# A macaron block on one core: routing in one tabled order, and float16 halves transposed by transfers

## The chip, the cores and the metric

The kernel runs on one core of a Trainium2 chip. The metric is the device time of one execution in microseconds; the figure for the kernel before is a median of three runs, 2352.42 us (2351.3 to 2353.59). Engines are named as the profile names them: PE (TensorE matmuls), PEld (its weight loads), DVE (VectorE), ACT (ScalarE), POOL (GpSimd) and SP (SyncE, which here only issues transfers).

## The reference

The input x is [2, 4096, 512] in float32. Three residual steps follow one another:

```python
x = x + 0.5 * ffn(layernorm(x))      # 1: routing, GRU, and alpha @ values
x = x + attn(layernorm(x))           # 2: gated delta rule over 4096 tokens
x = x + 0.5 * ffn(layernorm(x))      # 3: same weights as 1

def ffn(x):                          # 64 slots, hidden 256, top 8
    ctx = concat([x, mean(S)])                        # S: the 64 slots
    h = gelu(ctx @ w1.T + b1)
    logits = (h @ w2.T + b2) / (abs(tau) + 0.1)
    alpha = softmax over the 8 largest logits, 0 elsewhere
    slot_input = alpha.T @ x / alpha.sum(tokens)      # needs all tokens
    S_new = GRU(slot_input, S)
    return alpha @ (S_new @ wv.T + bv) @ wo.T + bo

def attn(x):                         # 16 heads of 32
    q, k = l2norm(x @ Wq), l2norm(x @ Wk); v = x @ Wv
    a, b = sigmoid(x @ Wa + ba), sigmoid(x @ Wb + bb)
    # per token: error = v - state k; state = a state + (b error) k; y = state q
    return (rmsnorm(y, g_norm) * silu(x @ Wg)) @ Wo
```

The slots' new values depend on every token of a batch, so each FFN is a pass that routes all tokens, a short GRU, and a second pass that adds `alpha @ values` to x. The second pass of step 1 is merged into the attention, that of step 3 is the end of the kernel.

## The kernel before, in words

The tokens go in 32 blocks (`NBLK`) of 128 tokens for each of the two batches (`NB`), so a block is a tile of 128 partitions by 2 x 512 float32, 512 KB. The stages follow each other: the routing of the first FFN (`ffn_a_phase(..., "a", ...)`), its GRU (`gru`), the attention (`attention`), the routing of the second FFN (the same function with "c"), its GRU, and the last pass (`after_c`).

**Products in halves.** Products that need float32 are made from float16 halves: a value is scaled and split into `hi`, its float16 rounding, and `lo`, the rounding of what is left. `mm3` issues three float16 matmuls for one product, L128 (hi x hi), L129 (hi x lo) and L130 (lo x hi), so these three lines carry all such products whatever stage they belong to. Weights are split once by `split16`: an ACT activation (L176) for the high half and a DVE operation (L177) for the low one.

**Routing.** It runs in ten groups of blocks (`split_blocks`: one block, seven groups of four, two, one). A group has six stages. `a_load` reads x. `a_stats` makes mean and variance on DVE. `a_norm` normalizes on DVE, casts the high half `xh` on ACT (L383) and subtracts the low half `xl` on POOL (L385). The hidden layer contracts over the 512 features, so it needs both halves feature-major, with features on partitions: for each block 16 PE transposes of 128 x 128 (L394) write to PSUM (`fpt`), and ACT (L397, high) and DVE (L399, low) copy them to `xTh` and `xTl`. `a_hidden` makes the hidden layer (`mm3`), its gelu on ACT (L417) and the logits. `a_topk` finds the top 8 and the softmax (DVE L431 to L458, an exponential on ACT, one addition on POOL). `a_slots` transposes alpha, keeps it (`alpha_out` stores it to HBM for the attention, `alpha_keep` keeps it in SBUF), and adds alpha.T @ x to sums in PSUM.

The order in which these stages of different groups are issued comes from fractions: each stage is a generator that yields how far it has come, each has a start and an end in units of a group (the dictionary `PA`), and `run_merged` keeps the generators on a heap and always advances the one that is earliest. Each engine executes its own instructions in the order of issue. The weights' setup (`setup_hidden`, `setup_gh`, `setup_attention`) is merged into the first routing in the same way (`extra_a`). All loads and stores of the routings are issued on SP's queue.

**Attention.** It is a software pipeline over the 32 blocks. `run_pipe` walks through a table (`PIPE`, 287 steps), where `qk0.5` means: advance the generator of stage `qk0` for the block five ahead of the current one by one step. Inside `tc.manual_schedule()` that is the order of issue. The stage `load` reads x and alpha. `prep` adds the first FFN's result to x (`ffn_b`: two matmuls, L488 and L489, and a DVE addition), stores x1, and makes the LayerNorm; then, for each batch, four float32 PE transposes (L814) fill a PSUM tile `apt`, ACT casts it to `xTh` (L816) and DVE subtracts to get `xTl` (L818). `qk0`, `qk1` and `vg` are the projections (L128 to L130). `post0`, `post1`, `bpart`, `decays`, `xk`, `dx`, `kk`, `dec`, `solve` and `chain` are the delta rule in chunks of 32 tokens. `tail` normalizes y by a square root on ACT, multiplies by Wo (L1080, tiles `apo`), adds the residual (DVE L1083) and stores x2. XK, Vt, Gt and x1 are read back from HBM on SP's queue, behind the stores that come before them in the order of issue. In PSUM three buffers of tag `pj` are shared by the projections, `ffn_b` and `apo`.

**Last pass.** `KEEP` blocks of x2 stay in SBUF from the second routing; the others are read again, `F3X` buffers of them, `F3L` blocks ahead.

Of the kernel before, what the change touches and what calls it, by code (L numbers as in the profile page):

```python
# [19 lines left out]
P = 128  # L20
D = 512
# [13 lines left out]
HEAD, TAIL = 1, 1  # L35
CFG = {"a": dict(XT=7, XN=2, XH=10), "c": dict(XT=4, XN=2, XH=11)}
KEEP = 12
F3A, F3X, F3L = 4, 11, 8
# [14 lines left out]
def split_blocks(n):  # L53

    cuts = [0] + list(range(HEAD, n - TAIL, GB)) + [n - TAIL, n]
    cuts = sorted(set(cuts))
    return [(a, b - a) for a, b in zip(cuts, cuts[1:])]


def run_merged(items):  # L60

    heap = [(s0, i, None) for i, (s0, s1, g) in enumerate(items)]
    heapq.heapify(heap)
    while heap:
        _, i, g = heapq.heappop(heap)
        s0, s1, f = items[i]
        if g is None:
            g = f()
        try:
            heapq.heappush(heap, (s0 + next(g) * (s1 - s0), i, g))  # L70
        except StopIteration:
            pass


def run_pipe(tc, stages, n):
# [3 lines left out]
    for w in PIPE.split():  # L79
        w, _, m = w.partition("*")  # L80
        name, lead = w.split(".")
        order += [(name, int(lead))] * int(m or 1)
    live = {}
    with tc.manual_schedule():
        for k in range(-max(lead for _, lead in order), n):
            for name, lead in order:
                t = k + lead
                if 0 <= t < n:
                    if (name, t) not in live:
                        live[name, t] = stages[name](t)  # L90
                    next(live[name, t], None)


@with_exitstack
def tile_macaron(
# [82 lines left out]

    isc1 = cp.tile([P, 1], F32, tag="isc1", name="isc1")
# [51 lines left out]
    def setup_gh(gp, big, ppj):  # L231
# [3 lines left out]
        whht = big.tile([P, KC, 3 * D], F32, tag="big", name="whht")  # L235
        for k in range(KC):
            nc.sync.dma_start(whht[:, k], whh[k * P:(k + 1) * P])
# [3 lines left out]
        nc.sync.dma_start(bsum, bhh.rearrange("(k p) -> p k", p=P))  # L241
        V.tensor_tensor(bsum[:, 0:8], bsum[:, 0:8], bihn[:, 0:8], ALU.add)
        ghb = gp.tile([P, 12, NS], F32, tag="ghb", name="ghbs")
        yield 0.1
        for g in range(12):
            pg = ppj.tile([P, NS], F32, tag="tr", name=f"pgh{g}")
            for k in range(KC):
                nc.tensor.matmul(pg, whht[:, k, g * P:(g + 1) * P], hsT[:, k], start=(k == 0), stop=(k == KC - 1))
            V.tensor_scalar(ghb[:, g], pg, bsum[:, g:g + 1], None, ALU.add)
            yield 0.1 + 0.9 * (g + 1) / 12  # L250
        nc.sync.dma_start(ghd, ghb)

    def setup_attention(gp, big, ppj):
# [5 lines left out]
        yield 0.1  # L259
        scales(gp, ppj, [s1[:, :, 0:2 * D], s1[:, :, 2 * D:]], scA[:, 0:2], iscA[:, 0:2], "wq")  # L260
        yield 0.3
        for k in range(KC):
            for s, i in ((slice(0, 2 * D), 0), (slice(2 * D, NQ), 1)):
                o = [W[n_][:, k, s] for n_ in ("wqh", "wql")]
# [903 lines left out]
```

## Time and profile before

| what | value |
| --- | --- |
| median of three runs | 2352.42 us |
| profiled execution, its own time | 2342.8 us |
| span of its instructions | 2341.0 us |
| mean granted TensorE clock | 0.960 |
| PE busy | 2100.5 us (90%) |
| PEld busy | 1585.4 us (68%) |
| DVE busy | 1911.3 us (82%) |
| ACT busy | 1148.9 us (49%) |
| POOL busy | 808.5 us (35%) |
| DMA traffic | 302.75 MB, mean 129 GB/s |
| first routing, its GRU | 0 to 275, to 301 us |
| attention | 301 to about 2003 us |
| second routing, its GRU | 2004 to 2252, to 2280 us |
| last pass | 2280 to 2341 us |

The profile is one execution. Its page gives busy time by engine, a strip of the span in 40 slices with a digit for the busy tenths of each (PEclk: the clock that was granted to PE), and groups of instructions by line: busy time, mean duration in ns, and then the idle time just before them on their engine with what ended it. Engines overlap, so shares don't add up to the span. A matmul's duration overlaps that of its neighbours.

### The profile page before, as it was taken

The page shows a single profiled execution, that of the slowest core. Times are in us where ns is not written, and L with a number is a line of the kernel's source. Part 1 is how long each engine was busy: PE and PEld are TensorE (multiplying, and loading weights), DVE is VectorE, ACT ScalarE, POOL GpSimd, SP SyncE. Part 2 cuts the span into 40 slices and gives each one's busy share as a digit, 9 for nine tenths or more (in the row PEclk, how much of TensorE's full clock was granted, in tenths as well). Part 3 has the DMA queues.
Part 4 walks back from the last instruction along what each step waited for, and adds up shares of the span by engine and source line. Part 5 has one row for each costly group of instructions (what it writes and reads, how often), then busy time and mean ns, then how long its engine had stood idle before and what let it go on. Part 6 is the DMA issues. An engine that isn't in the chain of part 4 may idle for free. (4 is left out here: it accounts for less than half of the span.)

```text
span 2341.0 us, 101047 instructions
## 1 busy us (share of the span) xinstructions
PE 2100.5 (90%) x44989; PEld 1585.4 (68%) x44989; DVE 1911.3 (82%) x4876; ACT 1148.9 (49%) x1957; POOL 808.5 (35%) x750
## 2 busy tenths in 40 slices
PE   5878878999999999999999999999999976588886
PEld 5767757767777676777767677777667754377774
DVE  7898538988888888888889888888888886489656
ACT  4677445544445444444545444554444421367631
POOL 2333114433334343333434333444333441134300
PEclk9898989999999999999999999999999988799997
DMA  6332323344443344343334444344444332630049
GB/s 212 123 127 91 96 87 129 119 133 130 142 134 126 123 136 132 128 150 121 126 124 139 128 136 148 120 127 132 135 128 146 102 97 70 219 110 29 2 149 368
DMA packets 176516, 302.75 MB, mean 129 GB/s; under 512 B 27984, under 2 KB 73552, under 8 KB 176080
## 3 DMA queue, kind: packets, MB, share of 16 engines
q1 hardware_dynamic: 161728, 256.45, 32.9%
q10 hardware_dynamic: 14352, 39.85, 5.2%
q8 instruction: 352, 5.77, 1.2%
q14 instruction: 84, 0.69, 0.1%
HBM read 189.23 MB, written 107.00 MB: 127 GB/s over the span
## 5 line engine op out<-in xcount | busy, mean ns | idle before, releaser
L1080 PE MATMUL apo<-wo,Gt 128*128 128x512 f32 x512 | 279.1, 630 | 24.5 <-DVE x1r L1083 24.5
L128 PE MATMUL pv<-xTh,wgh 128*128 128x256 f16 x1024 | 282.1, 275 | 0.0
L129 PE MATMUL pv<-xTh,wgl 128*128 128x256 f16 x1024 | 280.2, 274 | 0.1
L130 PE MATMUL pv<-xTl,wgh 128*128 128x256 f16 x1024 | 280.3, 274 | 0.0
L1014 POOL TENSOR_TENSOR ps<-ST,AC 128x256 f32<-128x256 f32 x128 | 105.5, 824 | 442.4 <-DVE ST L1038 442.4
L128 PE MATMUL pq<-wqh,xTh 128*128 128x384 f16 (+1 forms) x768 | 242.8, 316 | 1.5 <-issue 0.8
L129 PE MATMUL pq<-wqh,xTl 128*128 128x384 f16 (+1 forms) x768 | 240.9, 314 | 0.2 <-DVE xTl L818 0.2
L130 PE MATMUL pq<-wql,xTh 128*128 128x384 f16 (+1 forms) x768 | 240.7, 313 | 0.0
L862 POOL TENSOR_TENSOR qk<-qk,rn 128x512 f32<-128x512 f32 x128 | 137.6, 1075 | 231.7 <-issue 106.7
L836 ACT ACTIVATE qk<-pq,iscA 128x384 f32<-128x384 f32 (+1 forms) x192 | 105.4, 549 | 162.5 <-PE pq L130 139.5
L980 POOL TENSOR_TENSOR KQ<-KQ,Ax 128x512 f32<-128x512 f32 x128 | 168.4, 1315 | 0.4 <-PE pa L959 0.4
L764 DVE TENSOR_TENSOR tmp<-N,MT 128x256 f32<-128x256 f32 (+7 forms) x384 | 161.2, 426 | 5.6
L758 DVE TENSOR_TENSOR tmp<-N,U 128x256 f32<-128x256 f32 (+7 forms) x384 | 164.0, 434 | 1.4
L838 ACT ACTIVATE sq<-pq,iscA 128x384 f32<-128x384 f32 (+1 forms) x192 | 164.7, 858 | 0.0
L1018 PEld LDWEIGHTS pc<-KQ,S 32*32 32x32 f32 x8192 | 123.2, 106 | 50.6 <-ACT Y L1044 31.0
L760 DVE TENSOR_REDUCE MT<-tmp 128x32 f32<-128x256 f32 (+7 forms) x384 | 153.8, 407 | 0.0
L959 PE MATMUL pa<-KQ 32*32 32x64 f32 x8192 | 143.6, 217 | 11.2 <-ACT KQ L872 4.9
L1018 PE MATMUL pc<-KQ,S 32*32 32x64 f32 x8192 | 142.8, 217 | 9.5 <-DVE S L1040 4.9
L959 PEld LDWEIGHTS pa<-KQ 32*32 32x32 f32 x8192 | 121.7, 105 | 37.9 <-issue 14.9
L1035 PEld LDWEIGHTS pc<-X,u 32*32 32x32 f32 x8192 | 120.7, 105 | 38.6 <-issue 21.9
L1035 PE MATMUL pc<-X,u 32*32 32x64 f32 x8192 | 141.9, 216 | 5.2 <-ACT u L1032 3.7
L917 ACT ACTIVATE vg<-pv,iscA 128x512 f32<-128x512 f32 x128 | 88.1, 688 | 96.7 <-PE pv L130 88.7
(304 smaller groups left out, 5760.3 us busy)
## 6 DMA issues: line engine op xcount, KB each, us to landing
d<-a0d ACTq DMA_DIRECT2D x32, 528.0 KB
Ax<-a0d ACTq DMA_DIRECT2D x32, 528.0 KB
xt<-in_x_dram SPq DMA_DIRECT2D x32, 512.0 KB
x<-in_x_dram SPq DMA_DIRECT2D x64, 256.0 KB
x1d<-x SPq DMA_DIRECT2D x64, 256.0 KB
vtd<-vg SPq DMA_DIRECT2D x64, 256.0 KB
kd<-qk SPq DMA_DIRECT2D x64, 256.0 KB
XK<-kd SPq DMA_DIRECT2D x256, 64.0 KB
```

The costliest lines, as they stand in the source:

```text
L128: nc.tensor.matmul(po, lh, rh, start=start, stop=False, skip_group_check=True)
L129: nc.tensor.matmul(po, ll, rh, start=False, stop=False, skip_group_check=True)
L130: nc.tensor.matmul(po, lh, rl, start=False, stop=stop, skip_group_check=True)
L758: V.tensor_tensor(tv, vw(f, o10 + j0, [[C, n], [0, h], [1, ni]]), vw(U, ou + j0 * 17, [[0, n], [16, h], [1, ni]]), ALU.mult)
L760: yield lambda tv=tv, j0=j0: V.tensor_reduce(vw(mt, n * j0, [[1, n], [n, h]]), tv, AX.X, ALU.add)
L764: V.tensor_tensor(tv, vw(f, o11 + r0 * C, [[C, h], [0, n], [1, nk]]), vw(mt, 0, [[0, h], [n, n], [1, nk]]), ALU.mult)
L838: nc.scalar.activation(sq[:, f0:f1].rearrange("p (q g e) -> p q e g", g=NG, e=C), pq[:, 0:f1 - f0].rearrange("p (q e g) -> p q e g", g=NG, ...
L959: nc.tensor.matmul(pa[s, m], KQ[s, 0, c, b, g], KQ[s, :, c, b, g], start=(m == 0), stop=True, skip_group_check=True, tile_position=(32 * q ...
L980: nc.gpsimd.tensor_tensor(kc, kc, bass.AP(Ax.tensor, Ax[:, :, c].offset, [list(a[0]), [1, 2], list(a[1]), [1, C]]), ALU.mult)
L1018: nc.tensor.matmul(pcv[s, b, g, 0:2 * C], S[s, b, g], KQ[s, :, c, b, g], start=(g == 0), stop=False, skip_group_check=True, tile_position=tp)
L1035: nc.tensor.matmul(pcv[s, b, g, C:3 * C], u[s, b, g], d["X"][s, :, m], start=False, stop=True, skip_group_check=True, tile_position=tp)
L1080: nc.tensor.matmul(po, Gt[:, k, b], wo[:, k], start=(k == 0), stop=(k == KC - 1))
```

## The change

It has eight parts.

1. Both routings are issued by `run_pipe` with a table, `ROUTE`: 102 steps for a group (4 of load, 10 of stats, 24 of norm, 28 of hid, 20 of topk, 16 of slots), inside `tc.manual_schedule()`. `run_merged` and `PA` go. The setup of the weights is merged in between the steps (`extra`). The groups become one block, three, six of four, three, one: ten again.
2. In `a_norm` the 16 PE transposes of a block and their two copies out of PSUM go. Two `nc.sync.dma_start_transpose` per block, one of `xh` and one of `xl` (128 x 1024 float16, 256 KB each), write the feature-major tiles from SBUF to SBUF.
3. In the attention's `prep` the eight float32 PE transposes of a block go, with ACT's cast and DVE's subtraction from PSUM. ACT casts the token-major tile, POOL subtracts the low half, and four `dma_start_transpose` of 128 KB per block are issued on SP's queue.
4. The attention's weights are split by `split16p`: ACT scales in place, ACT copies the high half, POOL subtracts the low one. DVE has no part in it any more.
5. The routings' loads of x and of x2 and the stores of alpha are issued on ACT's queue.
6. PSUM in the attention: two buffers for the projections in place of three, and one of its own (`ppo`) for `ffn_b`, `pr` and `apo`. Most pools get `reuse_waits="tile"`, and a new pool `we` takes a part of the attention's tiles.
7. Sizes: `XT` 7 in both routings (4 in the second before), `XH` 9 (10 and 11 before), `KEEP` 11, `F3X` 14, `F3L` 11.
8. `PIPE` is a new table of 289 steps.

```diff
-HEAD, TAIL = 1, 1
-CFG = {"a": dict(XT=7, XN=2, XH=10), "c": dict(XT=4, XN=2, XH=11)}
-KEEP = 12
-F3A, F3X, F3L = 4, 11, 8
+HEAD, TAIL = (1, 4), (4, 1)
+CFG = dict(XT=7, XN=2, XH=9)
+KEEP = 11
+F3A, F3X, F3L = 4, 14, 11
...
+    def split16p(hi, lo, src, s):
+
+        nc.scalar.mul(src, src, s)
+        nc.scalar.copy(hi, src)
+        nc.gpsimd.tensor_tensor(lo, src, hi, ALU.subtract)
...
-                items += extra(gp, ptr, gw, NBLK / GB)
-                run_merged(items)
+                run_pipe(tc, stages, ng, ROUTE, extra(gp, ptr, gw, ng))
...
             nc.scalar.copy(xh, xn)
-            yield (j + 0.2) / blocks[1]
+            yield
+            nc.sync.dma_start_transpose(xTh, flat(xh))
+            yield
             nc.gpsimd.tensor_tensor(xl, xn, xh, ALU.subtract)
-            yield (j + 0.4) / blocks[1]
-            xTh = wp.tile([P, KC, NB * P], F16, tag="xTh", name=f"fxTh{u}", bufs=3)
-            xTl = wp.tile([P, KC, NB * P], F16, tag="xTl", name=f"fxTl{u}", bufs=3)
-            d["xT"].append((xTh, xTl))
-            for src16, dst, eng in ((xh, xTh, 0), (xl, xTl, 1)):
-                pt = ptr.tile([P, KC, NB * P], F16, tag="tr", name=f"fpt{u}_{eng}")
-                for k in range(KC):
-                    for b in range(NB):
-                        nc.tensor.transpose(pt[:, k, b * P:(b + 1) * P], src16[:, b, k * P:(k + 1) * P], ident16)
-                    yield (j + 0.4 + 0.3 * eng + 0.07 * (k + 1)) / blocks[1]
-                if eng == 0:
-                    nc.scalar.copy(dst, pt)
-                else:
-                    V.tensor_copy(dst, pt)
-                yield (j + 0.7 + 0.3 * eng) / blocks[1]
+            yield
+            nc.sync.dma_start_transpose(xTl, flat(xl))
+            yield
...
-        nc.sync.dma_start(xt, xr[t * P:(t + 1) * P])
+        nc.scalar.dma_start(xt, xr[t * P:(t + 1) * P])
...
-        nc.sync.dma_start(ald[t], aT.bitcast(F32))
+        nc.scalar.dma_start(ald[t], aT.bitcast(F32))
...
-            nc.sync.dma_start(xt, x2d[t * P:(t + 1) * P])
+            nc.scalar.dma_start(xt, x2d[t * P:(t + 1) * P])
...
+        ppo = pool("a1o", 1, space=PSUM)
         ptr = pool("a1t", 2, space=PSUM)
-        ppj = pool("a1p", 3, space=PSUM)
+        ppj = pool("a1p", 2, space=PSUM)
...
-                po = ffn_b(ppj, d["aT"], b, f"a{t}")
+                po = ffn_b(ppo, d["aT"], b, f"a{t}")
...
-                pt = ptr.tile([P, KC, P], F32, tag="tr", name=f"apt{t}_{b}")
-                for k in range(KC):
-                    nc.tensor.transpose(pt[:, k], xs[b][:, k * P:(k + 1) * P], ident)
-                yield
-                nc.scalar.copy(xTh[:, :, b], pt)
-                yield
-                V.tensor_tensor(xTl[:, :, b], pt, xTh[:, :, b], ALU.subtract)
+                xh = we.tile([P, D], F16, tag="xh", name=f"xh{t}_{b}", bufs=2)
+                nc.scalar.copy(xh, xs[b])
+                yield
+                nc.sync.dma_start_transpose(xTh[:, :, b], xh)
+                yield
+                xl = we.tile([P, D], F16, tag="xl", name=f"xl{t}_{b}", bufs=2)
+                nc.gpsimd.tensor_tensor(xl, xs[b], xh, ALU.subtract)
+                yield
+                nc.sync.dma_start_transpose(xTl[:, :, b], xl)
                 yield
...
-                po = ppj.tile([P, D], F32, tag="pj", name=f"apo{t}_{b}")
+                po = ppo.tile([P, D], F32, tag="pj", name=f"apo{t}_{b}")
```

## The prediction

> **What bounds the kernel now.** First the page's strips, for the stages.
>
> ```profile
> PE   5878878999999999999999999999999976588886
> DVE  7898538988888888888889888888888886489656
> PEclk9898989999999999999999999999999988799997
> DMA  6332323344443344343334444344444332630049
> ```
>
> Each digit is 58.5 us. Routing of the first FFN fills about the first five, the second's the five before the last two; in between is the attention, with PE at 9 throughout. The view by windows (columns: stretch, its length, busy PE, weight loads, DVE, ACT, POOL, granted clock, DMA share, GB/s) puts numbers on it:
>
> ```profile
> 0.00:275.00 275.00, 211.72 (x2491) 189.46 (x2491) 225.10 (x612) 172.85 (x245) 84.59 (x56) 0.92 0.37 123
> 25.00:275.00 250.00, 207.27 (x2472) 185.39 (x2472) 211.57 (x572) 168.44 (x239) 82.98 (x45) 0.91 0.33 108
> 477.00:1800.00 1323.00, 1294.62 (x32323) 937.53 (x32327) 1158.16 (x2918) 642.06 (x1171) 520.33 (x520) 1.00 0.41 132
> 2004.00:2252.00 248.00, 192.63 (x2370) 169.59 (x2370) 186.03 (x528) 158.78 (x220) 83.37 (x46) 0.89 0.23 82
> 2089.00:2199.00 110.00, 90.25 (x1175) 80.60 (x1176) 96.88 (x269) 82.50 (x112) 46.40 (x23) 0.97 0.06 21
> ```
>
> 477 to 1800 is the attention in its steady state: 26 blocks of 50.9 us, PE busy 98%, DVE 88%. So PE sets it. 2089 to 2199 is the second routing's steady state: 16 blocks (128 of its 256 L394 transposes) of 6.9 us, and there DVE leads with 88%, PE has 82%, ACT 75%. The first routing has DVE at 85% over 250 us. Third, the groups by shape, for what goes:
>
> ```profile
> L814 PE MATMUL apt<-ident,x 128*128 128x128 f32 x256 | 38.9, 275 | 10.0 <-ACT x L810 10.0
> L816 ACT CAST xTh<-apt 128x512 f16<-128x512 f32 x64 | 37.5, 586 | 57.4 <-PE pv L129 35.6 <-PE apt L814 21.7
> L818 DVE TENSOR_TENSOR xTl<-apt,xTh 128x512 f16<-128x512 f32 x64 | 43.7, 683 | 29.6 <-ACT xTh L816 21.5 <-PE pv L130 8.1
> L399 DVE COPY fxTla<-fpta 128x1024 f16<-128x1024 f16 x32 | 21.9, 686 | 15.5 <-PE fpta L394 15.4
> L397 ACT COPY fxTha<-fpta 128x1024 f16<-128x1024 f16 x32 | 32.3, 1010 | 4.9 <-PE fpta L394 4.7
> L385 POOL TENSOR_TENSOR xla<-fxna,xha 128x1024 f16<-128x1024 f32 x32 | 69.0, 2162 | 119.6 <-ACT xha L383 108.5 <-DVE s1a L448 11.1
> L177 DVE SCALAR_TENSOR_TENSOR wql<-wq,scA,wqh 128x256 f16<-128x256 f32 x16 | 13.8, 967 | 0.0
> L177 DVE SCALAR_TENSOR_TENSOR wgl<-wg,scA,wgh 128x512 f16<-128x512 f32 x8 | 6.7, 859 | 0.0
> ```
>
> A matmul's own 275 ns overlaps its neighbours. What a transpose takes of PE's stream is seen in the timeline, from its start to the next one's:
>
> ```profile
> 1002.12 0.60 PE L814 MATMUL apt<-ident,x 128*128 128x128 f32 x4
> 1002.55 0.29 PE L128 MATMUL pq<-wqh,xTh 128*128 128x288 f16 x1
> ```
>
> Four take 0.43 us; another set (1024.49 to 1025.02) 0.53.
>
> **The change part by part.** *Attention.* Eight transposes a block leave PE: 0.43 + 0.53 = 0.96 us, 31 us over 32 blocks. DVE loses 2 x 0.68 = 1.4 us a block, so it goes from 44.5 to 43.1 of 50 and doesn't take over. ACT casts from SBUF in place of PSUM: half of a 1.05 us L383 cast, 0.53 against 0.59, nothing. POOL gains two subtractions of half L385's size, 2.2 us on 20 of 50.9; it is hidden by its 30 idle us, and if it weren't the 2.2 would show in full. Four transfers of 128 KB join SP's queue, each behind its cast or subtraction; behind them wait the stores of qk, v and gate and the loads of XK, Vt, Gt and x1. SP idles in waits for most of its time now, so a late transposing input costs only where such a load is late already: DVE waits 44.7 us in all for x1r at L1083. By the new table the first half lands some 30 of 289 steps (5 us) before its first matmul, the second about 50 steps (9 us). PSUM goes from three shared buffers to two for the projections and one for the output matmuls; PE waits on L1083 for that buffer today (23.5 us in the steady state), and I expect that to change hands, not to go. I take the 31 us.
>
> *Second routing.* DVE loses L399 (0.68 of its 96.88 / 16 = 6.05 us a block), leaving 5.37. At the share of today, 88%, a block takes 6.10, 0.77 less: 25 us over 32. ACT's 5.16 loses 1.01 and gains a load's issue, 0.33: 4.5, hidden under DVE. PE loses 16 transposes of about 55 ns. At its start, the x2 loads stand on SP behind the last store of the attention; DVE waits 9.5 us for the first. In the changed order they stand on ACT, right behind the tail's last square root (1991 us now, 14 us earlier), so this wait can go; the transposing way to the first hidden layer is a little longer than 1.03 us of PE and 1.01 of ACT. I take 7.
>
> *First routing.* DVE's 225.1 loses 21.9 (L399) and 21.4 (L177: 13.8, 6.7 and 0.9 for small pieces): 182. ACT's 172.9 loses 32.3, gains the in-place scaling (same shapes as L176's 11.4, 5.4 and 1.2: 18.0) and 64 issues of 0.33 (21): 180. POOL gains 8,320 elements a partition at L385's 2.11 ns: 17.6 on 84.6, hidden. With two engines level, ACT's 168.4 - 32.3 + 18 + 21 = 175 at the 85% that DVE has today fills 206 of the 250 us: -44. ACT never reaches that share now (67%), so I take 40.
>
> *The rest.* One x2 block more is read again (KEEP 11): 0.5 MB at the last window's 353 GB/s, +1.5. The 102 pieces and the finer release of buffers have no row of their own: between -25 (a routing whose DVE stalls fall from 12 to 5%, both FFNs) and +25 (they grow as much); taken at 0.
>
> *The price of a transposing transfer* is in no row. The page's row of the hardware queue has packets, MB and the share of 16 engines' time:
>
> ```profile
> q1 hardware_dynamic: 161728, 256.45, 32.9%
> ```
>
> Below: 256.45 MB in 32.9% of 2341 us is 333 GB/s, so 256 KB take 0.8 us. Above: that queue's mean packet takes 76 ns (0.329 x 2341 x 16 / 161,728); one such for each of 1,024 source rows of 128 halves, over 16 engines, is 4.9 us. Same bytes, same engines, both ends on chip: nearest to the first; I take 1.6. A routing block has two, 3.2 us of DMA in 6.1, hidden. [...]
>
> **Sum.** -31 - 25 - 7 - 40 + 1.5 = -101.5. The profiled execution took 2342.8 us (span 2341.0), so 2241.3 in its terms; the median, 2352.42, lies 9.6 above it: 2251.
>
> **The rivals.** *The transposes become the bound* (slower). Place: SP's queue and the 16 engines in both routings, two a block. For: they are issued by one queue in order, and hidden matmuls three buffers on wait for them. Against: 0.8 us at the ordinary rate, and DMA at 0.33 and 0.06 of its time. At the upper price 64 x 4.9 = 314 us a phase; with 25 and 20 us of filling, the routings take 339 and 334 in place of 275 and 248: +64 + 86 - 31 = 2471. They bind above 3.0 us each, and the whole becomes slower where 128 T + 45 exceeds 275 + 248 + 31, above 4.0.
>
> *The new attention table gives the PE time back.* PE's gaps are only 28.4 us of 1323, but single waits (L1083's 1.8 us) show how one misplaced evacuation stalls the stream, and the projections have one PSUM buffer less. One microsecond a block more cancels the 31: 2282; two: 2314; from three a block on, 2346, the whole gains nothing. Against: tail and block preparation use the single buffer in turn, never at once.
>
> *The tables do better than the shares of today.* PE's idle 1.1 us a block goes (-35), both routings run DVE at 95% (-15, -15): 2186.
>
> **Chances.** Sum as above 0.42; gain given back 0.17, of which 0.04 with three microseconds a block or more; tables better 0.13; transposes bound 0.26, nearly all of it above 4.0 us each, since a price that binds is one near the upper end; no net effect 0.02. A difference of 0.2% (4.7 us) is about what can be told. Faster: 0.42 + 0.13 + 0.13 = 0.68; same 0.03 (no net effect and 0.01 of the 0.04); slower 0.26 + 0.03 = 0.29. The range runs from the third rival's 2186 up into the first one's, to 2400, where a transpose takes 128 T + 45 = 554 + 48, so T = 4.35 us.
>
> **What would show it.** Right: attention blocks near 49.9 us with no L814; second routing near 6.1 us a block, DVE still above 85%; transposes landing within 5 us; PE's waits for xTl small. Wrong: PE or weight loads waiting on DMA xTh, xTl, fxTh or fxTl, SP busy with the transposes' issue for more than half of a routing, blocks of the attention at 51 us or more.

## The result, and the profile after

The changed kernel takes 2379.03 us (median of five, 2367.97 to 2389.4) against 2353.59 for the kernel before: a ratio of 1.010, with a 95% interval of 1.0059 to 1.014. It is 1.1% slower by the medians, where 4.3% faster was forecast. The profiled execution took 2389.4 us, its span is 2387.6. It is the slowest of the five, while the profiled execution of the kernel before (2342.8 us) is faster than any of the five that its median is from: the 46.6 us between the two profiles below are 25.4 us between the medians.

The view by windows of the changed kernel, cut at the last matmul or the first one of each stage (columns as in the prediction), gives routing, GRU, attention, second routing, GRU and last pass:

```profile
0.00:318.30 318.30, 202.40 (x1978) 172.47 (x1979) 188.95 (x550) 166.89 (x248) 104.70 (x84) 0.86 0.65 158
318.30:350.30 32.00, 27.62 (x145) 21.54 (x146) 13.29 (x44) 5.84 (x11) 0.67 (x4) 0.77 0.44 150
350.30:2055.40 1705.10, 1595.75 (x39458) 1141.42 (x39457) 1478.39 (x3523) 878.36 (x1504) 682.67 (x708) 0.97 0.48 135
2055.40:2299.80 244.40, 174.96 (x1858) 148.81 (x1856) 155.70 (x495) 133.10 (x186) 80.22 (x46) 0.84 0.71 152
2299.80:2329.00 29.20, 24.41 (x148) 19.65 (x147) 13.62 (x42) 5.40 (x13) 0.00 (x0) 0.89 0.92 336
2329.00:2387.60 58.60, 34.90 (x128) 23.00 (x128) 40.08 (x67) 10.96 (x28) 0.00 (x0) 0.83 0.93 350
```

Cut in the same way, the kernel before has 274.1, 26.9, 1698.8, 250.4, 29.7 and 61.1. So the 46.6 us between the spans are +44.2 and +5.1 in the first routing and its GRU, +6.3 in the attention, -6.0 in the second routing, -0.5 and -2.5 at the end. In the first routing no engine is at its limit any more: PE has 64% of 318 us, DVE 59% (82% of 274 before), ACT 52%, POOL 33%. The stage waits, and it is seen in the strips too, where DVE is at 4 to 7 at the start instead of 5 to 9:

```profile
PE   3867679899999999999999999999999987478775
DVE  4667543998999999989899999998989896467646
PEclk9879778999999999999999999999999996679998
DMA  7667345445544445555445545455454431568769
```

What it waits for is in the waits of the first routing (engine, tile and line, what ended the wait: sum in us, times, longest one), and one round of it in the timeline of ACT and DVE:

```profile
PE fpha L129 <- ACT hTa L421: 29.8, 27, 2.9
PE fpha L129 <- DMA fxTha<-xha: 14.3, 3, 6.6
DVE frsa L375 <- ACT frsa L373: 27.6, 7, 12.2
ACT hTa L421 <- PE fpha L131: 96.9, 38, 15.1
```

```profile
56.78 0.56 ACT L421 ACTIVATE hTa<-fpha,hb,isc 128x256 f32<-128x256 f32 x1 [2.34 <-PE fpha L131]
58.91 0.56 ACT L421 ACTIVATE hTa<-fpha,hb,isc 128x256 f32<-128x256 f32 x1 [1.56 <-PE fpha L131]
59.49 1.28 ACT L373 ACT_TABLE_LOAD   x1
60.78 0.30 ACT L373 ACTIVATE frsa<-fmva,epsx 128x8 f32<-128x8 f32 x1
61.11 0.20 DVE L375 RECIPROCAL frsa<-frsa 128x8 f32<-128x8 f32 x1 [12.20 <-ACT frsa L373]
```

A group's square root (L373) stands on ACT behind four gelus of an earlier group (the four between 50.92 and 59.5). Each gelu waits for PE (2.34 and 1.56 us for the last two); PE itself had waited 5.13 us for a transposing transfer just before, and then for the gelus. Meanwhile DVE, whose normalization would feed the next transfer, issues nothing for 12.2 us. In the kernel before ACT waited 22.7 us for the hidden layer's matmuls (L417) where it now waits 96.9, and DVE waited once for a square root, 1.1 us. PE's granted clock was lower too: 0.86 in the first routing, where it is busy for 64% (0.92 and 77% before), and 0.84 in the second at 72% (0.90 and 77%); the first routing's hidden matmuls take 313 ns on average instead of 288 (but 314 in route_free below, which is 36 us shorter there).

In the attention the steady state is 50.73 us a block (50.80 before; mean of 25 steps between the first output matmuls of successive blocks, which is what "a block" means below). The L814 transposes are gone, but PE's largest wait has only changed its name. In the waits of the kernel before over 26 blocks it was this:

```profile
PE apo L1080 <- DVE x1r L1083: 23.5, 26, 1.8
```

In those of the changed kernel, over 26 blocks too, it is a wait of the same size for another evacuation:

```profile
PE kqt L887 <- POOL qk L880: 24.3, 27, 2.1
```

And all of PE's waits together have grown, as the window of those blocks shows:

```profile
530.00:1851.00 1321.00, 1275.98 (x32181) 914.91 (x32172) 1199.15 (x2863) 715.02 (x1226) 550.15 (x572) 1.00 0.50 142
```

PE is idle for 45.0 us here, for 28.4 in the kernel before (the prediction's row from 477 to 1800). Per block its busy time fell from 49.7 to 49.0 us and its idle time rose from 1.1 to 1.7.

The second routing lost at its start. From its first hidden matmul to that of the fifth block it takes 44 us, where route_free below takes 21. DVE stands still for a square root there again (the window from 2066 to 2114 us):

```profile
DVE frsc L375 <- ACT frsc L373: 18.7, 2, 11.7
```

From the 13th block to the 29th a block takes 6.2 us (7.1 in the kernel before), with DVE busy for 71%:

```profile
2165.40:2264.40 99.00, 78.28 (x929) 69.33 (x928) 70.58 (x225) 64.61 (x92) 38.74 (x21) 0.95 0.83 166
```

The transposing transfers themselves are quick. In SP's timeline of the second routing each of these two is a stretch of 1.23 us in which the queue only issues it:

```profile
2174.88 1.23 SPq L399 DMA_TRANSPOSE fxThc<-xhc  x1
2177.09 1.23 SPq L403 DMA_TRANSPOSE fxTlc<-xlc  x1
```

Two transfers of 256 KB that had the engines nearly to themselves, issued at 85.44 us and at 2174.88 us, moved 1,024 packets of 256 bytes each. The first packet started 1.17 us after the start of the issue, the last one ended 1.1 and 1.4 us later (244 and 185 GB/s), and the completion was signalled 2.7 and 3.1 us after the start of the issue.

### The profile page after: what moved, and what is told of

It is laid out like the page before. It is cut to its first block, busy times and chain, and to the rows that moved or that the text cites. A ratio compares the mean times of both kernels' runs of the same rounds, so it can differ in the third digit from the quotient of the medians.

```text
span 2387.6 us, 98974 instructions
## 1 busy us (share of the span) xinstructions
PE 2060.0 (86%) x43709; PEld 1526.9 (64%) x43709; DVE 1890.0 (79%) x4720; ACT 1200.6 (50%) x1990; POOL 868.3 (36%) x842
## 5 line engine op out<-in xcount | busy, mean ns | idle before, releaser
L1003 POOL TENSOR_TENSOR X<-XK,Dx 128x256 f32<-128x256 f32 x128 | 100.7, 787 | 590.6 <-DMA XK<-kd 530.7
L1099 PE MATMUL apo<-wo,Gt 128*128 128x512 f32 x512 | 262.4, 617 | 1.8 <-DVE x1r L1102 1.3
L774 DVE TENSOR_TENSOR tmp<-N,U 128x256 f32<-128x256 f32 (+7 forms) x384 | 196.6, 526 | 4.7
L780 DVE TENSOR_TENSOR tmp<-N,MT 128x256 f32<-128x256 f32 (+7 forms) x384 | 186.8, 493 | 4.6
L999 POOL TENSOR_TENSOR KQ<-KQ,Ax 128x512 f32<-128x512 f32 x128 | 160.1, 1251 | 2.4 <-PE pa L977 2.4
L1054 PE MATMUL pc<-X,u 32*32 32x64 f32 x8192 | 147.7, 219 | 12.5 <-issue 8.7
```

The costliest lines, as they stand in the source:

```text
L774: V.tensor_tensor(tv, vw(f, o10 + j0, [[C, n], [0, h], [1, ni]]), vw(U, ou + j0 * 17, [[0, n], [16, h], [1, ni]]), ALU.mult)
L780: V.tensor_tensor(tv, vw(f, o11 + r0 * C, [[C, h], [0, n], [1, nk]]), vw(mt, 0, [[0, h], [n, n], [1, nk]]), ALU.mult)
L999: nc.gpsimd.tensor_tensor(kc, kc, bass.AP(Ax.tensor, Ax[:, :, c].offset, [list(a[0]), [1, 2], list(a[1]), [1, C]]), ALU.mult)
L1054: nc.tensor.matmul(pcv[s, b, g, C:3 * C], u[s, b, g], d["X"][s, :, m], start=False, stop=True, skip_group_check=True, tile_position=tp)
L1099: nc.tensor.matmul(po, Gt[:, k, b], wo[:, k], start=(k == 0), stop=(k == KC - 1))
```

## The experiments

Theory 1 was that the way through SP and the DMA engines delays the routings; theory 2, that the new order of issue does. All runs in one table. Stages are those of the profiled execution; "first" is the end of the first routing, "second" the length of the second. Equal routings differ from one execution to another by up to 5 us (first: 315.1 to 319.7 with the kept order) and up to 14 (second: 239.5 to 253.4), and the same attention took 50.80 us a block in the kernel before and 51.01 in best1.

| run | first | attention, us a block | second | ratio to before (95%) |
| --- | --- | --- | --- | --- |
| before | 274.1 | 50.80 | 250.4 | |
| changed | 318.3 | 50.73 | 244.4 | 1.010 (1.006 to 1.014) |
| new_pe | 376.9 | 51.72 | 301.0 | 1.075 (1.071 to 1.079) |
| old_dma | 269.9 | 52.15 | 240.4 | 1.010 (1.006 to 1.014) |
| low_dve | 345.3 | 54.26 | 253.4 | 1.061 (1.055 to 1.068) |
| gelu_after | 340.5 | 51.82 | 276.3 | 1.048 (1.045 to 1.052) |
| sqrt_early | 330.5 | 50.59 | 263.0 | 1.029 (1.025 to 1.033) |
| best1 | 267.3 | 51.01 | 247.0 | 0.992 (0.990 to 0.995) |
| old_route | 274.7 | 50.69 | 235.5 | 0.991 (0.988 to 0.993) |
| route_free | 282.5 | 50.73 | 226.0 | 0.990 (0.987 to 0.993) |
| free_split | 279.5 | 50.63 | 234.7 | 0.995 (0.993 to 0.997) |
| no_xl | 315.1 | 50.64 | 239.5 | 1.011 (1.007 to 1.015) |
| best2 | 268.4 | 50.59 | 235.6 | 0.987 (0.983 to 0.990) |
| best3 | 266.5 | 50.52 | 234.1 | 0.990 (0.987 to 0.992) |
| prep_early | 267.2 | 53.22 | 233.7 | 1.014 (1.011 to 1.016) |
| att_free | 319.7 | 64.78 | 249.0 | 1.192 (1.188 to 1.196) |
| xtb3 | 269.8 | 52.80 | 236.2 | 1.017 (1.013 to 1.020) |
| best2x3 | 266.6 | 50.59 | 232.4 | 0.985 (0.983 to 0.988) |
| xk_early | 266.1 | 52.53 | 235.8 | 1.012 (1.009 to 1.014) |
| repaired | 285.3 | 52.16 | 228.7 | 1.014 (1.011 to 1.017) |

**Order or transfers: new_pe, old_dma.** new_pe is the changed kernel with its transposes back on PE, old_dma the kernel before with transfers in their place and with the routings' loads and the stores of alpha on ACT's queue.

```diff
 new_pe
-            nc.sync.dma_start_transpose(xTh, flat(xh))
+            pt = turn(xh, 0)          # 8 PE transposes into PSUM, then a copy
 old_dma
-                    for b in range(NB):
-                        nc.tensor.transpose(pt[:, k, b * P:(b + 1) * P], src16[:, b, k * P:(k + 1) * P], ident16)
+            nc.sync.dma_start_transpose(xTh, flat(xh))
```

> The changed kernel with its new orders, queues, buffers and weight split, but with all transposes back on PE: in the routings 16 per block with the copies out of PSUM on ACT (high half) and DVE (low half), in the attention eight float32 ones per block with ACT's cast and DVE's subtraction. The stages are read one by one. Theory 1 (the way through SP and the DMA engines is what delays): the first routing ends near 274 to 285 us instead of 318, and the second takes 245 to 255 us; the attention, with the transposes' 1 us a block back on PE, takes 51.5 to 52 us a block. Theory 2 (the new order of issue is what delays, square roots and normalizations standing behind gelus): the first routing still ends after 305 us, DVE still waits over 20 us for the square root; the attention stays at 50.9 us or more.

> The kernel before with its old orders, buffers and weight split, but with the transposes of both routings and of the attention done by transposing transfers on SP's queue, as the change does it, and the routings' loads on ACT's queue. Theory 1 (the transfers are what delays): the first routing ends at 300 us or later and hidden matmuls wait for fxTh and fxTl; the attention takes over 51 us a block. Theory 2 (the new order is what delays): the first routing ends at 274 us or earlier, the second takes 240 us or less, and the attention takes 49.9 to 50.5 us a block, since PE has lost its 1 us.

In the routings theory 1 fell at once. With the old order the transfers shorten both, to 269.9 and 240.4; with the new order and no transfers they last 376.9 and 301.0, which is also far more than theory 2 needed (the copies out of PSUM now stand in an order made without them). In the attention the four corners are 50.80 (old table, PE), 52.15 (old table, transfers), 51.72 (new table, PE) and 50.73 (new table, transfers). Under the new table the transfers are worth 0.99 us, about what the prediction has PE lose (0.96), but that table, with its split of PSUM and its pools, costs 0.92 without them. Most of it is idle time of PE, 1.9 us a block in new_pe and 1.1 in the kernel before:

```profile
590.00:1940.00 1350.00, 1300.07 (x32356) 934.37 (x32353) 1227.44 (x2924) 714.04 (x1225) 491.54 (x524) 1.00 0.40 129
```

Under the old one the transfers come late, as PE's largest wait in the steady state of old_dma says:

```profile
PE pq L129 <- DMA xTl<-xl: 41.9, 24, 2.4
```

**The order, part by part: old_route, best1, route_free.** best1 is the kernel before with the routings' transposes by transfers, and with their loads and the stores of alpha on ACT's queue; nothing else. old_route is the changed kernel's attention and weight split with the old order in the routings. route_free changes one thing: the routings' table is walked outside the region that keeps its order on every engine, so that the framework's scheduler may move instructions of an engine ahead of others, as it may in the kernel before. It does move them: DVE's instructions of the first routing come in another order than in the changed kernel, while att_free below, which keeps that order, has the same sequence to the instruction.

```diff
 route_free
-    with tc.manual_schedule():
+    with tc.manual_schedule() if manual else ExitStack():
...
-                run_pipe(tc, stages, ng, ROUTE, extra(gp, ptr, gw, ng))
+                run_pipe(tc, stages, ng, ROUTE, extra(gp, ptr, gw, ng), manual=False)
```

> The kernel before with one part of the change alone: the transposes of both routings by transposing transfers on SP's queue, and the routings' loads and the stores of alpha on ACT's. Orders, sizes, weight split and the attention stay as before. From the run with the old order: first routing ends at about 270 us (274 before), the second takes 240 to 244 us (250 before). Theory 1 would have both slower than before; theory 2 has the whole at 2325 to 2332 us of span, 0.4 to 0.7% faster than before.

> The changed kernel's attention (new table, transfers, PSUM and pools) and its weight split by ACT and POOL, with the old order, groups and sizes in the routings, whose transposes are transfers. If the weight split is what slows the first routing, it ends at 290 us or later; if the order does, it ends at 265 to 272 us. The attention should again take 50.7 us a block and 1705 us in all, whatever the routing is; the second routing 231 to 242 us. The whole: span 2320 to 2335 us if the order is the cause, 2345 or more if the weight split is.

> The changed kernel with one edit: the routings' table of 102 steps is walked outside the region in which the order of issue is kept on each engine, so that the framework's scheduler may put instructions of an engine ahead of others, as it does in the kernel before (the attention's table keeps its order). All steps, sizes, transfers and queues stay. Theory 2a (keeping the table's order on every engine is what costs): the first routing ends at 270 to 285 us instead of 318, the second takes 225 to 240 us. Theory 2b (the groups, sizes and steps of the table are what costs, not that their order is kept): the first routing still ends after 305 us. The attention stays at 50.7 us a block in both.

All three are faster than before. route_free is decisive, since it keeps table, groups, sizes, queues and transfers: the first routing goes from 318.3 to 282.5, the second from 244.4 to 226.0, the whole from 1.010 to 0.990. Over all runs whose edits leave them alone, first routings with the kept order end at 315.1 to 319.7 us and second ones take 239.5 to 253.4; freed, they have 279.5 to 285.3 and 226.0 to 234.7. The ranges lie 30 us apart in the first and 5 in the second, where the means differ by 17. old_route has 274.7 where 265 to 272 was expected of the order alone; the weight split below may have a part in that. In its waits the square root falls to 6.5 us and ACT's wait for the hidden layer to 69.3:

```profile
DVE frsa L375 <- ACT frsa L373: 6.5, 2, 3.8
ACT hTa L421 <- PE fpha L131: 69.3, 32, 6.7
PE fpha L131 <- DMA fxTla<-xla: 17.8, 9, 3.5
```

PE's waits for the transfers don't fall (17.8 us for the low halves, 11.1 with the kept order). They are there, and they are not what cost.

**Single waits in the kept order: gelu_after, sqrt_early.** With the order kept, each of the two most visible waits was taken away by itself: the second half's matmuls that stand behind the first half's gelu, and the square root behind the gelus.

```diff
 gelu_after
-                nc.scalar.activation(hT[:, hc], ph[:, hc], AF.Gelu, bias=hb[:, hc:hc + 1], scale=isc1)
-                yield
+            for hc in range(2):
+                nc.scalar.activation(hT[:, hc], ph[:, hc], AF.Gelu, bias=hb[:, hc:hc + 1], scale=isc1)
+                yield
...
-        ppo = pool("a1o", 1, space=PSUM)
-        ppj = pool("a1p", 2, space=PSUM)
+        ppo = ppj = pool("a1p", 3, space=PSUM)
 sqrt_early: the 9th of a group's 10 "stats" steps stands behind the 8th in ROUTE;
             the attention's pools without reuse_waits
```

> The changed kernel with two edits in stages that are read apart. Routings: both gelu steps of a block come after all 24 matmuls of its hidden layer, as in the kernel before, so that the second half's first matmul no longer waits for the first half's gelu (the halves share one PSUM tile); steps and transfers as in the changed kernel. Attention: the projections and the output matmuls share three PSUM buffers again. Theory 4 (the round trip from PE to ACT and back in every half paces the routings): the second routing, 231 us from its first hidden matmul to its last slot matmul, takes 205 to 215, and the first, 290 us, takes 250 to 265. Rival (DVE's normalization behind square roots, or the transfers, pace it): both change by less than 6 us. Attention: if the split of PSUM costs the new table its gain, 50.0 to 50.3 us a block in place of 50.7; if not, 50.6 to 50.9 or more.

> The changed kernel with two edits in stages that are read apart. Routings: in the table the square root of a group's statistics moves 22 steps forward, right behind the last statistics, so that it stands ahead of three gelus on ACT; its reciprocal stays where it is. Attention: the pools without the finer release of buffers (the option reuse_waits is left out). Theory 5 (DVE's normalization waits behind gelus for the square root, 27.6 and 22.8 us): the second routing falls from 231 to about 212 us from its first hidden matmul on, the first from 290 to about 265, and the wait for frs goes. Rival (theory 4, the gelu's round trip): the wait for frs goes, another takes its place, and both fall by less than 8 us. Attention: 50.7 us a block if the option does nothing there, over 51 if it does.

Both theories fell, and both routings got longer by 12 to 32 us. In gelu_after PE now waits 48.2 us in the first routing for the gelus before the logits; in sqrt_early the square root's wait is gone from DVE's list, and DVE waits 34.7 us (15.6 before the edit) for the exponential on ACT. In an order that is kept on five engines and the queues, taking one wait away by itself lengthened others. In the attention, PSUM in one pool costs 1.1 us a block, so the split is worth having under the new table; the finer release of buffers is worth nothing there (50.59).

```profile
PE pla L426 <- ACT hTa L422: 48.2, 43, 3.4
```

That was the wait of gelu_after's first routing, the next is that of sqrt_early's:

```profile
DVE lga L451 <- ACT lga L449: 34.7, 8, 8.9
```

**Weights and low halves: low_dve, no_xl, free_split.**

```diff
 low_dve
-                nc.gpsimd.tensor_tensor(xl, xs[b], xh, ALU.subtract)
+                V.tensor_tensor(xl, xs[b], xh, ALU.subtract)
...
-        nc.gpsimd.tensor_tensor(lo, src, hi, ALU.subtract)
+        V.tensor_tensor(lo, src, hi, ALU.subtract)
 no_xl
-                nc.gpsimd.tensor_tensor(xl, xs[b], xh, ALU.subtract)
-                nc.sync.dma_start_transpose(xTl[:, :, b], xl)
+                nc.sync.dma_start_transpose(xTl[:, :, b], xh)
 free_split: route_free with split16 in place of split16p
```

> The changed kernel with the low halves subtracted on DVE instead of POOL in two places: xl of the attention (two of 0.7 us a block) and the attention's weights in the first routing (split16p). Theory 3 (POOL's added subtractions run beside DVE's small operations and double those, 418 to 970 ns): the attention falls under 50.5 us a block although DVE gets 1.4 us more of its own; the operations tmp of 256 elements are back near 425 ns. Rival (the table sets the pace, PE waiting for qk of POOL): the attention stays at 50.9 or rises by up to 1 us. First routing: if POOL's part of the weight split holds the transposes back (SP waits 19.5 us for it), it ends 10 to 20 us earlier; if not, within 5 us of 318.

> The changed kernel without POOL's subtraction of the attention's low half: the second transfer of each half moves the high half once more, so the low half of the attention's input is left out of the result's meaning, while every transfer, matmul and step stays. Theory 3a (POOL's 2.3 us of subtractions a block, with the DVE operations of two SBUF inputs that wait beside them, took back PE's microsecond): the attention falls from 50.7 to 49.8 to 50.2 us a block, the wait of PE for qk of POOL shrinks to under half of 24 us, and DVE's tmp operations of 256 elements are at 425 ns throughout. Rival (the fixed order sets the pace through other waits): 50.5 us a block or more. The routings stay as in the changed kernel.

> The changed kernel with the routings' table not kept on each engine, as in the run before it, and the attention's weights split on ACT and DVE as in the kernel before (split16) instead of ACT and POOL. If the weight split costs the first routing time (274.7 us with the old order and the split on POOL, 267 to 270 without), it ends 4 to 8 us earlier than 282.5; if POOL's part is hidden, within 2 us of it or later. Second routing 226 us, attention 50.7 us a block, as before.

The subtractions on DVE make the attention 3.5 us a block longer, more than the 1.4 us of two subtractions at L818's 683 ns in the kernel before and more than either side expected, and the first routing 27 us longer (345.3), which neither side expected. no_xl leaves out the low half of the attention's input and is good for its times only: without POOL's subtraction the attention stays at 50.64. So POOL's share in the low halves doesn't set the pace, and in this order DVE is the worse place for it. The weight split by POOL costs the first routing 3 us with the freed order (282.5 to 279.5) and about 6 with the old one (274.7 in old_route; 267.3 in best1, 269.9 in old_dma, and 268.4 in best2, which also has the finer release). free_split as a whole is not faster than route_free (0.995 and 0.990), so the 3 us can't be told from the spread between executions.

**Where the attention's microsecond went: prep_early, xtb3, best2x3, xk_early, repaired, att_free.** Each edit is against one suspected wait. prep_early, under the old table, has all `prep` and `load` steps one block earlier. xtb3 and best2x3 give the transfer to `xTh`, for whose buffer SP waits 340.0 us in the changed kernel's steady state, a third buffer, under the old and under the new table. xk_early moves two steps that load XK, for which POOL waits 459.5 us in the steady state of the changed kernel (never in the kernel before), and repaired does so together with route_free's edit. att_free walks the attention's table outside the region that keeps order.

```diff
 prep_early: every prep.N and load.N of the old PIPE as N+1, XTB = 3
 xtb3, best2x3
-    XTB, QKB, YB, XRB = 2, 2, 2, 1
+    XTB, QKB, YB, XRB = 3, 2, 2, 1
 xk_early, repaired
-  ... xk.4 solve.3 kk.4 ... tail.2 xk.4 ... vg.5 xk.4
+  ... xk.4*3 solve.3 kk.4 ... tail.2 ... vg.5
 att_free
-        run_pipe(tc, stages, NBLK, PIPE)
+        run_pipe(tc, stages, NBLK, PIPE, manual=False)
```

> The routings of the best version; in the attention the old table, PSUM and pools, with transposing transfers, and the stages load and prep one block earlier in the table (every prep.N and load.N as N+1, three buffers of xTh and xTl instead of two). The order within a block of the pipeline stays; the halves land a block before they are used. Theory 6 (PE's microsecond is there, the old table only gave the transfers too little lead): the wait of PE for xTl, 41.9 us in the run with the old order, goes, and the attention falls from 52.15 to 49.7 to 50.2 us a block; the whole ends near 2295 to 2305 us of span. Rival (the pace is set by other waits of the fixed order): the wait for xTl goes, another of about 1 us a block takes its place, and the attention takes 50.6 us a block or more.

> The changed kernel with both the routings' and the attention's table walked outside the region that keeps their order on each engine. Theory 7 (keeping an order costs in the attention as it did in the routings): the attention falls under 50.3 us a block. Rival (the attention's table is worth its keeping): over 52 us a block. Routings as in the run without their fixed order: 280 to 285 us, and 226 to 235.

> The routings of the best version, and in the attention the old table with its leads as they were and transposing transfers, with three buffers of xTh and xTl instead of two; nothing else. Theory 8 (the transfer that waits for a buffer blocks SP's queue, and what stands behind it comes late): SP's wait after PE's pv falls from 8 us a block to under 2, PE's wait for xTl from 1.6 us a block to under 0.8, and the attention from 52.15 to 50.0 to 51.0 us a block. Rival (the halves are late because of cast and subtraction, not of the queue): the wait for the buffer goes, and the attention stays within 0.3 us of 52.15.

> The best version (old order in the routings, the changed kernel's attention) with three buffers of xTh and xTl in the attention instead of two. Theory 8: SP's wait after PE's pv, 340 us in the changed kernel, goes, x1 and Gt land earlier, and the attention falls from 50.6 to 49.8 to 50.3 us a block, the span from 2319 to 2300 to 2310. Rival (under the new table PE waits for POOL's qk, which SP's queue doesn't carry): within 0.2 us of 50.6 a block.

> The best version (old order in the routings, the changed kernel's attention) with one edit in the attention's table: the third and the fourth step of xk, which load the second half of XK, stand right behind the second one (67 and 118 steps earlier). Theory 9 (XK lands late, POOL waits for it, qk stands behind it and PE waits for qk): POOL's wait for XK falls from 489 to under 150 us of the steady state, PE's wait for qk from 22 to under 8 us, and the attention from 50.6 to 49.7 to 50.2 us a block; span 2295 to 2308 us. Rival (POOL's wait is idle time that no one needs; DVE's rn or another wait takes over): POOL's wait falls, PE's waits stay about 1 us a block in all, and the attention takes 50.4 us a block or more.

> The changed kernel with two edits: the routings' table not kept on each engine, and the two loading steps of xk moved forward as in the other run. Theory 9: first routing 280 to 285 us, attention 49.7 to 50.2 us a block, span 2308 to 2320 us, 1.2 to 1.7% faster than before. Rival: attention 50.4 or more a block and a span of 2330 to 2340 us, as without the second edit.

Every theory fell. The rivals had the direction, but not always the size: xtb3's 52.80 us a block is outside the 52.15 and 0.3 either way of its rival, and repaired's span of 2384.6 us is far above the 2330 to 2340 of its own. PE's largest wait in the steady state of prep_early is one for DVE's x1r:

```profile
PE apo L1097 <- DVE x1r L1100: 64.1, 26, 3.9
```

In that of best2x3 the largest is still the one for qk:

```profile
PE kqt L889 <- POOL qk L882: 26.5, 25, 2.4
```

In that of xk_early it is the low half's transfer, and next a wait for DVE:

```profile
PE pq L145 <- DMA xTl<-xl: 41.4, 26, 2.5
PE pc L1049 <- DVE TT L1014: 33.3, 21, 1.9
```

In prep_early the wait for xTl is gone, and DVE's x1r, whose load stands behind the transfers on SP, is late by 2.5 us a block instead. In xtb3 SP no longer waits for the buffer, yet the low halves are late as before (PE waits 35.1 us for them). In best2x3, too, SP no longer waits for the buffer, and PE still waits for qk. In xk_early XK comes earlier (POOL's wait falls from 489.1 us in best2 to 266.7), and now the transfers of the low half, behind it on SP, are late by 1.6 us a block: they are issued 10.1 us (median) after their subtraction, 7.9 in best2. In att_free only the attention was freed: the edit did not reach the routings, whose 319.7 and 249.0 us are those of a kept order. There the attention takes 64.78 us a block, so for this table keeping the order is worth 14 us a block, while for the routings' table it costs.

**Versions that beat both: best2, best3, best2x3.** best2 has the old order in the routings with transfers, weights split on ACT and DVE, the changed attention, and the finer release of buffers in the routings' pools. best3 takes the second routing from route_free.

> A version put together from what has been seen: old order, groups and sizes in the routings, with transposing transfers; weights split on ACT and DVE as before; the attention of the changed kernel; and the finer release of buffers in the routings' pools, so that the second routing's first loads need not wait for all of the attention's buffers. First routing 267 to 270 us, attention 1705, second routing 220 to 232 in place of 235.5 (its first hidden matmul 15 to 25 us after the attention instead of 31). Span 2310 to 2325 us, 1 to 1.5% faster than before.

> The best version so far (old order in the first routing, transposing transfers in both, weights split on ACT and DVE, the attention of the changed kernel, finer release of buffers) with the second routing taken from the changed kernel, its table not kept on each engine. First routing 268 us, attention 1701 to 1705, second routing 226 in place of 235.6. Span 2307 to 2315 us, 1.6 to 2% faster than before. If the second routing gained only from a later start, it stays at 235 us and the span at 2319.

best2 takes 2323.19 us (median), 0.987 of before; with a third buffer (best2x3) 2319.97, 0.985 (0.983 to 0.988), the lowest of all, though the two intervals overlap. The finer release did not bring the second routing's start forward as expected (its first hidden matmul comes 28.3 us after the attention, 31.1 before), and best3's second routing came to 234.1, not 226: what looked like a gain of the freed table over the old order lies within the spread of that stage.

## Why the prediction was wrong

**The order was taken at nothing.** The step that failed is "The 102 pieces and the finer release of buffers have no row of their own", which the prediction bounds by 25 us either way and takes at 0. Keeping the table's order on each engine cost 36 us in the first routing (318.3 against 282.5) and some 10 to 18 in the second (244.4 against 226.0 to 234.7). By the medians of the whole kernel it is 47 us (2379.03 against 2332.24): about twice the upper end. The bound was made from DVE's stalls as they stood, 12% of the stage; but in the kept order the engines waited for one another (in the first routing ACT 96.9 us for PE, PE 29.8 and DVE 27.6 for ACT), and DVE was idle for 41% of it.

**First routing, -40.** Even with the order out of the way it came to 4 to 7 us (269.9, 267.3, 268.4 against 274.1). In these three runs DVE lost its copies (21.9 us) but kept the weight splits; in old_route it lost both, and the stage took 274.7, no gain at all. So moving the splits, for which the sum takes 21.4 us off DVE, brought nothing. The step that failed is filling time by the busiest engine: "at the 85% that DVE has today". DVE was busy but did not set the pace; in best2 it has 208.08 of 268.4 us, 78%. What sets it there stays open.

```profile
0.00:268.40 268.40, 185.66 (x1978) 163.49 (x1979) 208.08 (x578) 138.41 (x209) 84.03 (x56) 0.89 0.77 190
```

**Second routing, -25 and -7.** The 7 at its start were about right (9.4): the first hidden matmul comes 13.4 us after the attention instead of 22.8. The stage gained 6.0 us in all, so the kept order ate all but the start. Its middle has nearly the 6.1 us a block that was forecast, but not for the reason given: DVE is busy for 71% there, where the sum had 88%, and "still above 85%" was the sign of being right. That the number fits is luck. Without the kept order the stage gains 16 to 24 us of the 32 (226.0 to 234.7), with the old one and transfers 3 to 18 (247.0 in best1 to 232.4 in best2x3).

**Attention, -31.** The term had the right size, and the rival that gives it back had the right price. Transfers under the new table are worth 0.99 us a block (51.72 to 50.73), costed at 0.96; the new table, with its split of PSUM and its pools, costs 0.92 without them (50.80 to 51.72). The rival had "one microsecond a block more cancels the 31", by a misplaced evacuation or the PSUM buffer that is missing. That PE stalls more is shown (1.1 us of idle time a block before, 1.9 in new_pe), that one misplaced evacuation does it is not, and the PSUM part was wrong: the split helps by 1.1 us. The stage as a whole is 6.3 us longer, since its first output matmul comes 177.9 us after its start (153.6 before) and less than that is made good at the end. Which property of the new table costs the 0.92 is not settled; none of the edits against a single wait gave it back.

**The price of a transfer, 1.6 us.** It was 1.1 to 1.4 us of traffic, between the lower bound of 0.8 and the 1.6 taken, and the rival in which the transfers bind fell: the old order with transfers has shorter routings than the kernel before. What the bound left out is that SP is held about 1.23 us by each (medians of 1.23 us for 256 KB, 1.22 and 1.26 for 128 KB), and that in the two undisturbed ones 2.7 and 3.1 us passed until the transfer had landed.

**The rest.** POOL's subtractions in the attention stayed hidden as said (no_xl). The last pass got 2.5 us shorter instead of 1.5 longer (F3X and F3L were left out of the sum). The first GRU took 5.1 us more, which no step had; its clock was 0.77 instead of 1.00. It need not be the change's: the same stage takes 27.7 us in no_xl and in att_free.

## What to carry to other kernels

When a change fixes an order of issue, give it a term that can be as large as the stage's idle time, and not zero: count the places where an instruction that feeds another engine stands behind one that waits for PE, and remember that shares of busy time say nothing of a stage in which no engine is full. Change order and data path in separate steps: here the change was 1% faster without the kept order and 1% slower with it, and one line parts the two. In an order that is kept on every engine, each single wait taken away here came back elsewhere, so such an order is to be made anew after an edit rather than patched. And read a stage from its start: the second routing lost its time in the first four blocks, while its middle ran nearly as fast as forecast.

## What was not expected of the hardware

A DVE operation with two inputs in SBUF took 2.4 times as long beside one of POOL's. In the steady state of the changed kernel the multiplication tmp (128 x 256) takes 418 ns (median) where POOL is idle and 991 ns where POOL's subtraction xl runs (989 to 995, 26 times); those of this size with an input in PSUM (zt, NT, ST) have medians of 412 to 425 ns, beside a POOL operation or not. Each of the 26 starts 0.44 us after an xl and ends 0.28 us after that xl's end. The group of all 96 shows it as a mean; among the groups of the kernel before (busy us and mean ns behind the bar) it is

```profile
L758 DVE TENSOR_TENSOR tmp<-N,U 128x256 f32<-128x256 f32 x96 | 41.0, 428 | 1.1
```

and among those of the changed kernel

```profile
L774 DVE TENSOR_TENSOR tmp<-N,U 128x256 f32<-128x256 f32 x96 | 54.7, 598 | 1.2
```

What holds the slowed operations up is not shown. They still didn't set the pace: without xl the attention took 50.64 us a block, with it 50.73.

The way of a transposing transfer wasn't foreseen either. In the two undisturbed ones the first packet came only 1.17 us after the start of SP's issue, and between first and last packet they ran at 244 and 185 GB/s, below the 333 that the prediction works out for the queue in the kernel before.
